# Softmax sums of attention on VectorE, one-bank PSUM slots and shared SBUF slots in a four-layer graph network on one core

## The chip, the cores and the metric

The kernel runs on one core of a Trainium2 chip. The metric is the device time of one execution in microseconds. Before the change three runs gave 3714.34, 3720.96 and 3722.38 us; the median is 3720.96 us.

Each core has TensorE (PE: matrix products, fed by weight loads that overlap them), VectorE (DVE), ScalarE (ACT), GpSimd (POOL) and SyncE (SP, which here issues nearly all DMAs). Matrix products are written to PSUM, 8 banks of 2 KB per partition; everything else lies in SBUF.

## The reference

32 graphs of 512 nodes with 256 features pass through four layers. Each layer normalises its input, cuts it at zero, and adds its result to x:

```python
h = jnp.maximum(_layernorm(x, axis=-1), 0.0); x = x + L0(h, adj)  # 4 heads, additive scores
h = jnp.maximum(_layernorm(x, axis=-1), 0.0); x = x + L1(h, adj)  # 1 head, softmax over axis 1
h = jnp.maximum(_layernorm(x, axis=-1), 0.0); x = x + L2(h, adj)  # bilinear scores
h = jnp.maximum(_layernorm(x, axis=-1), 0.0); x = x + L3(h, adj)  # transformer block
```

Layer 3 is the one that matters most here. It has 8 heads of 32 columns:

```python
q, k, v = heads(split(x @ Wqkv.T + bqkv))
scores = where(allowed, einsum('bhqd,bhkd->bhqk', q * scale, k), -inf)
attn = softmax(scores, axis=-1)
ctx = einsum('bhqk,bhkd->bhqd', attn, v)
x = layernorm(x + ctx @ Wo.T + bo) ; x = layernorm(x + relu(x @ W1.T + b1) @ W2.T + b2)
```

A graph therefore has six norms: one before each layer and two inside layer 3.

## The kernel before, in words

Nodes lie in four blocks of 128 partitions. The program is a list of jobs, one list of the same jobs for each graph. A table, `PLACES`, holds one number for each job of a graph, in the order in which the source makes the jobs. Graph b's job i stands at b x 100,000 + PLACES[i], and `carry_out` emits all jobs of all graphs in the order of these places; on each engine this is the order of execution. So the jobs of about five graphs are interleaved, and a "round" of 100,000 places holds every job of one graph's list once, from different graphs. A job is one instruction, except that a call of `matmuls` is one job for a group of products. Each float32 product appears in the trace as two instructions. In the first rounds the later layers' work is not there yet, and in the last rounds the earlier layers' work is gone: these are called fill and drain below.

`WARM` is a second list: at a place it puts a number of products of the identity with a weight, whose results nobody reads (`ps_warm` in the trace). They stand only in the first rounds. Before, there are 78 of them.

Tiles are handed out of slots. `K` says how many slots each kind of tile has, and `carry_out` gives a new tile the slot that has been out of use longest. The eight PSUM banks before: `ps_a`, two slots of one bank; `ps_b`, two slots of two banks; `ps_ct` and `ps_to`, one bank each. In SBUF each kind of tile has its own slots: small numbers of columns aside, 14 slots of 2 KB (p, y, to, inv3), 23 of about 4 KB (x, masks, h, hT, wh and so on) and 6 of 8 KB (adj, rows0, p1, qk and two for p3).

`norm_stats` (L445) does four statistics and four aggregations on VectorE, then the inverse root of the variance: Ln and Exp on ScalarE, three VectorE steps of a Newton iteration, one VectorE check of range into `ok`, and `shift` on VectorE. `normed` applies it with four ScalarE instructions.

In layer 3 (L680) the heads come in two groups of four (loop over g), and for each group the source nodes come in four blocks (loop over j). For one (g, j): four products give the scores `ps_s` of four heads; two ScalarE exponentials of 1024 columns give `p3`; VectorE multiplies it with the mask; then four products with v add to `ps_ct`, and four products with a matrix of ones add to `ps_to`, the sum of the exponentials, spread over the 32 rows of each head. After j = 3 the sums of the first group go through DRAM to be turned into reciprocals in a shape that uses all partitions (`to_d`, `part`, `in_d`, `inv`: four DMAs in a row), and those of the second group are turned directly from PSUM by two VectorE reciprocals of 256 columns. The output projection `wo`, a norm, the feed-forward products (`ps_f`, first f1, then f2), and a last norm follow.

The late weights (13 tensors of layer 3, 16 loads) are put on GpSimd's queue behind the larger of the first two numbers of the table, that is behind the first loads of adjacency and x.

Of the kernel before, what the change touches and what calls it, by code (L numbers as in the profile page):

```python
# [11 lines left out]
F32 = mybir.dt.float32  # L12
# [4 lines left out]
OP = mybir.AluOpType  # L17
# [13 lines left out]
SHIFT = 45.0  # L31

# [250 lines left out]
def width(args):  # L283
# [7 lines left out]
    4941, 0, 45989, 55878, 52736, 53088, 65883, 75806, 126827, 257141, 153885, 318759, 211656, 217633, 19570,  # L291
    1228, 4500, 10919, 22752, 14242, 24780, 24734, 24972, 24973, 27735, 28443, 30996, 28846, 32925, 37040,
    40036, 39571, 47279, 52268, 53574, 53821, 53821, 54654, 43514, 54475, 54475, 54993, 55764, 55984, 55984,
    55984, 55984, 56107, 61238, 61239, 61239, 61239, 61300, 63031, 63709, 66485, 67354, 69503, 62835, 62835,
    67024, 64457, 65078, 68506, 69270, 74656, 76682, 80285, 83989, 77078, 81039, 86599, 86599, 86599, 89133,
    89469, 89469, 93130, 79369, 91586, 88558, 103135, 103216, 103216, 104243, 105108, 105108, 98449, 109305,
    108751, 106888, 109305, 109305, 109392, 109476, 111470, 112436, 115065, 110602, 104584, 113822, 117055,
    117056, 128079, 128539, 128539, 128540, 131428, 131985, 131985, 160167, 164815, 157449, 132402, 141909,
    138829, 164636, 146420, 163821, 163940, 170363, 172091, 172091, 178335, 195013, 352413, 196976, 205278,
    205507, 205507, 205507, 205306, 205742, 205742, 205751, 205972, 205777, 205777, 205829, 205829, 208425,  # L300
    213342, 214247, 214247, 208403, 208426, 208428, 210913, 210913, 213654, 209281, 209281, 210044, 218310,
    215531, 233659, 226926, 226927, 233310, 233310, 247338, 251067, 253705, 254637, 234450, 237759, 237759,
    242240, 233549, 235402, 241481, 252228, 239918, 242726, 247267, 254175, 257745, 257745, 257745, 257745,
    257745, 258204, 258204, 258204, 259293, 259293, 330297, 272806, 262275, 257879, 257938, 259931, 260558,
    258171, 257938, 261933, 260558, 262075, 262075, 262075, 265602, 265603, 267573, 265874, 269500, 269793,
    267082, 269953, 270582, 270582, 270871, 271669, 271669, 271613, 271613, 271613, 271805, 271805, 271670,
    273796, 273591, 273796, 273861, 276238, 278300, 279108, 279108, 279109, 279109, 279039, 274044, 276752,
    280924, 276983, 282260, 285040, 285625, 287505, 282260, 281913, 283149, 286565, 284076, 286699, 288031,
    288518, 288143, 281743, 281743, 281743, 282736, 282736, 290598, 302996, 303568, 304126, 289466, 291476,
    293111, 298737, 298738, 299315, 291986, 296584, 296584, 328450, 424820, 304255, 294640, 311427, 316750,  # L310
    316314, 305973, 313426, 317622, 318586, 318586, 319319, 319319, 320472, 317622, 321103, 325728, 328100,
    325395, 326602, 333285, 333285, 333677, 335177, 336098, 336215, 336215, 336215, 336215, 370706, 345694,
    351822, 351822, 351822, 352367, 354547, 353407, 353408, 355772, 355772, 356635, 355773, 341670, 341670,
# [15 lines left out]
]  # L329

WARM = [
    (86598, 15), (103134, 3), (109304, 4), (117054, 3), (143513, 8), (186598, 16), (203134, 3), (243513, 8),
    (253820, 2), (255983, 5), (262834, 2), (270581, 1), (273590, 2), (279107, 2), (281742, 1), (286598, 1),
    (341669, 2),
]
# [1001 lines left out]
```

## Time and profile before

| | |
|---|---|
| median of three runs | 3720.96 us |
| span of the profiled execution | 3722.8 us |
| PE busy | 3638.5 us |
| DVE busy | 2742.9 us |
| ACT busy | 1813.4 us |
| POOL busy | 11.1 us |
| `ps_to` products | 2048 instructions, mean 594 ns |
| `ps_ct` products | 2048 instructions, mean 605 ns |
| mask product `p<-p,m` of 128x2048 | 256 instructions, mean 2284 ns |
| exponential `p<-ps_s` of 128x1024 | 512 instructions, mean 1023 ns |

The profiled execution's span lies 1.8 us above the median. Products of four heads run beside each other in the array, and products are pipelined, so the cost of a group is read from the distance of its start to the next group's start, not from the mean of one instruction. In the busy table a share is of the whole span; in the rows of slices each digit is the busy share of a fortieth of the span in tenths.

### The profile page before, as it was taken

What the parts mean: (1) busy time and instruction counts of PE and PEld (TensorE: products, weight loads), DVE (VectorE), ACT (ScalarE), POOL (GpSimd) and SP (SyncE); (2) the same over time, 40 slices, a digit from 0 to 9 for tenths busy, and PEclk for the clock granted to TensorE, in tenths of its full rate; (3) what the DMA queues carried; (4) which work ended last, traced back from release to release, by engine and by line L of the source; (5) the groups of instructions that cost most, each with busy time, mean ns of one, the idle gap of its engine ahead of it and who ended that gap; (6) DMA issues with size and microseconds to landing.
All of it is one profiled execution on the core that took longest, in us unless ns stands there. A gap on an engine that the chain in (4) does not pass through costs nothing.

```text
span 3722.8 us, 52235 instructions
## 1 busy us (share of the span) xinstructions
PE 3638.5 (98%) x20130; PEld 2376.4 (64%) x20130; DVE 2742.9 (74%) x6267; ACT 1813.4 (49%) x3393; POOL 11.1 (0%) x25
## 2 busy tenths in 40 slices
PE   6899999999999999999999999999999999999986
PEld 5766676666666666666666667666667666666543
DVE  4687777787777787777788777778777778777554
ACT  1255544545544455544455554455554455554443
POOL 1000000000000000000000000000000000000000
PEclk8899999999999999999999999999999999999998
DMA  4111111111111111111111111111111111110000
GB/s 139 40 44 49 30 31 49 45 44 49 32 32 46 45 44 50 32 36 42 45 44 50 32 46 31 45 48 45 33 45 31 47 48 44 43 36 15 15 10 10
DMA packets 152351, 152.75 MB, mean 41 GB/s; under 512 B 87840, under 2 KB 122144, under 8 KB 148000
## 3 DMA queue, kind: packets, MB, share of 16 engines
q1 hardware_dynamic: 149632, 144.35, 13.4%
q0 software_dynamic: 1216, 3.94, 0.3%
q8 instruction: 161, 2.64, 0.3%
q10 hardware_dynamic: 1248, 1.05, 0.1%
q14 instruction: 94, 0.77, 0.1%
HBM read 114.57 MB, written 17.96 MB: 36 GB/s over the span
## 4 chain that ended last, share of the span: by engine, by line
PE 94%; DVE 3%; DMA 1%; ACT 1%; issue 0%; SPq 0%; ACTq 0%; DVEq 0%
PE ps_o L267 24%; PE ps_f L267 24%; PE ps_s L267 7%; PE ps_ct L267 6%; PE ps_wh L267 6%; PE ps_qk L267 6%; PE ps_to L267 6%; PE ps_t L265 4%; PE ps_e L267 4%; PE ps_v L267 3%; PE ps_wo L267 3%; DVE p L214 1%; DMA rows<-rows_d 1%; PE ps_y L265 1%; DVE st L214 0%
## 5 line engine op out<-in xcount | busy, mean ns | idle before, releaser
L267 PE MATMUL ps_o<-wh,p 128*128 128x65 f32 (+1 forms) x5120 | 723.8, 298 | 9.5 <-DVE p L214 9.1
L267 PEld LDWEIGHTS ps_o<-wh,p 128*128 128x128 f32 x5120 | 679.5, 194 | 76.7 <-issue 37.3
L214 DVE TENSOR_TENSOR p<-p,m 128x2048 f32<-128x2048 f32 x256 | 584.7, 2284 | 33.7 <-ACT p L214 33.7
L214 ACT ACTIVATE p<-ps_s 128x1024 f32<-128x1024 f32 x512 | 506.6, 1023 | 183.1 <-PE ps_s L267 182.3
L267 PE MATMUL ps_f<-tT,ff_t 128*128 128x512 f32 x1024 | 456.4, 599 | 2.6 <-ACT tT L214 2.6
L267 PE MATMUL ps_f<-ff_t,f 128*128 128x256 f32 x2048 | 454.1, 380 | 0.0
L267 PEld LDWEIGHTS ps_f<-ff_t,f 128*128 128x128 f32 x2048 | 384.4, 190 | 51.4 <-issue 1.8
L214 DVE SCALAR_TENSOR_TENSOR p<-rows,rt,mT 128x512 f32<-128x512 f32 x512 | 368.4, 738 | 18.3 <-DMA rows<-rows_d 18.3
L214 ACT ACTIVATE h<-x,shift,rstd 128x256 f32<-128x256 f32 x512 | 272.5, 590 | 215.5 <-PE ps_o L267 160.0
L267 PEld LDWEIGHTS ps_f<-tT,ff_t 128*128 128x128 f32 x1024 | 193.9, 192 | 222.6 <-issue 208.7
L267 PE MATMUL ps_s<-qk 32*128 32x512 f32 x2048 | 294.9, 641 | 2.5 <-ACT qk L214 1.4
L214 ACT ACTIVATE f<-ps_f,ff1b_c 128x512 f32<-128x512 f32 x256 | 164.0, 679 | 247.0 <-PE ps_f L267 247.0
L267 PE MATMUL ps_ct<-p,v 128*32 128x512 f32 x2048 | 272.9, 605 | 8.2 <-DVE p L214 7.0
L267 PE MATMUL ps_to<-p,ones 128*32 128x512 f32 x2048 | 267.5, 594 | 0.0
L214 ACT ACTIVATE rstd<-mv,eps 128x4 f32<-128x4 f32 x192 | 56.2, 292 | 432.9 <-DVE mv L214 432.8
L267 PE MATMUL ps_o<-h,p 128*128 128x257 f32 x1024 | 240.4, 387 | 0.0
L267 PE MATMUL ps_qk<-h3T,wqkv_t 128*128 128x512 f32 x512 | 238.3, 593 | 0.0
L267 PEld LDWEIGHTS ps_o<-h,p 128*128 128x128 f32 x1024 | 190.8, 191 | 52.3 <-issue 26.0
L214 DVE TENSOR_TENSOR u<-ps_f,n 128x512 f32<-128x512 f32 x64 | 44.3, 692 | 237.4 <-PE ps_f L267 237.4
L214 DVE BATCH_NORM_STATS2 st<-x 128x6 f32<-128x256 f32 x512 | 204.3, 415 | 9.1 <-DMA x<-in_x_dram 4.7
L267 PEld LDWEIGHTS ps_s<-qk 32*128 32x128 f32 x2048 | 81.4, 183 | 166.3 <-ACT p L214 55.4
L265 PEld LDWEIGHTS ps_t<-ident,h 128*128 128x128 f32 x1024 | 120.3, 142 | 93.5 <-issue 52.3
(133 smaller groups left out, 4489.3 us busy)
## 6 DMA issues: line engine op xcount, KB each, us to landing
adj<-in_adj_dram SPq DMA_DIRECT2D x32, 1024.0 KB
rows<-rows_d SPq DMA_DIRECT2D x32, 1024.0 KB
x<-in_x_dram SPq DMA_DIRECT2D x32, 512.0 KB
rows<-rows_d SPq DMA_DIRECT2D x32, 512.0 KB
out_dram<-y SPq DMA_DIRECT2D x32, 512.0 KB
inv<-in_d SPq DMA_DIRECT2D x32, 256.0 KB
ff_t<-in_L_gnn_W_dram POOLq DMA_DIRECT2D x2, 1024.0 KB, 11.8
mT<-m SPq DMA_TRANSPOSE x128
```

What stands on the lines that cost most here:

```text
L214: return [getattr(unit, method)(*map(real, args), **{k: real(v) for k, v in kw.items()})]
L265: made.append(self.nc.tensor.transpose(*map(real, c)))
L267: made.append(self.nc.tensor.matmul(*map(real, c[:3]), start=c[3], stop=c[4]))
```

## The change

The sums of the exponentials move: VectorE adds the four masked tiles of a head group into one tile `acc` (three additions of 128x2048), and one group of four products with ones turns `acc` into `ps_to`. The reciprocals of both head groups now go through DRAM. All PSUM tiles share eight slots of one bank; score tiles, projections and feed-forward tiles are made one bank wide, so an exponential now takes 512 columns and there are four per (g, j). SBUF tiles of layer and kind share slots by size: 9 of 8 KB, 19 of 4 KB, 8 of 2 KB. The inverse root is two GpSimd instructions (add, power of -0.5), without Newton steps. Range checks are gathered in one tile `seen` per graph and done by three instructions. Several steps go from VectorE to ScalarE: the mask tile `m`, the first half of the transposed copies, the layer 0 products `wh` (now one per head), and the layer 2 products `ha`. The adjacency of a graph is now issued ahead of its x. The whole table of places is new, and `WARM` has 276 products in 25 places.

Places in the new table that are spoken of below: adjacency load 0, x load 29304, first root of x 63434, `h0` transposes 70775 and after, scores of layer 3 from 385313 to 416057, the last sum 424877, ones-products 410801 and 427148, output projection 432396 to 440859, feed-forward products 448926 to 476873. (A place of 385313 is place 85313 of a graph's fourth round.)

```diff
-            adj=1, x=3, mT=3, m3=3, h0=1, h0T=1, wh0=1, rows0=1, e0=1, p=6,
-            h1=1, h1T=1, wh1=1, rows1=1, p1=1, y=4, x2=2,
-            h3=1, hT3=1, qk=1, vt=1, p3=2, to=2, inv3=2, n=1,
-            kinds=2, rt0=2, rt1=2, inv2=2, part=4,
...
-    K |= {"ps_ct": Kind(psum, "ps_ct", 1), "ps_to": Kind(psum, "ps_to", 1)}
-    K |= {"ps_a": Kind(psum, "ps_a", 2), "ps_b": Kind(psum, "ps_b", 2)}
+    SHARED = dict(
+        big="adj rows0 p1 qk p3 acc",
+        mid="x x2 mT m3 e0 h0 h0T wh0 h1 h1T wh1 rows1 h3 hT3 vt n",
+        half="p y to inv3",
+    )
+    K = {tag: Kind(act, tag, slots) for tag, slots in dict(big=9, mid=19, half=8).items()}
+    K |= {"ps": Kind(psum, "ps", 8)}
...
-        plan.act("activation", rstd, mv[:, :, 1], AF.Ln, bias=eps, fixed=0.27)
-        plan.act("activation", rstd, rstd, AF.Exp, scale=-0.5)
-        r = new("newton", "newton", [P, NT])
-        plan.dve("scalar_tensor_tensor", r, mv[:, :, 1], EPS, rstd, OP.add, OP.mult)
-        plan.dve("scalar_tensor_tensor", r, r, -0.5, rstd, OP.mult, OP.mult)
-        plan.dve("scalar_tensor_tensor", rstd, r, 1.5, rstd, OP.add, OP.mult)
-        plan.dve("scalar_tensor_tensor", ok[:, :NT], mv[:, :, 1], 2.0**60, ok[:, :NT], OP.is_le, OP.mult)
+        ve = new("ve", "ve", [P, NT])
+        plan.pool("tensor_scalar_add", ve, mv[:, :, 1], EPS, fixed=0.6)
+        plan.pool("tensor_tensor", rstd, ve, nhalf, OP.pow, fixed=0.6)
...
-        plan.dve("tensor_scalar_max", m, adj_t, 0, each=0.52e-3)
+        plan.act("activation", m, adj_t, AF.Relu, fixed=0.5)
...
-            if k % 2:
-                plan.act("copy", hT[:, k], to_sbuf)
-            else:
-                plan.dve("tensor_copy", hT[:, k], to_sbuf)
+            plan.act("copy", hT[:, k], to_sbuf)
...
-            plan.dve(
-                "tensor_mul",
-                wh[:, i, :, :F0],
-                ps[:, :D].split("p (h f) -> p h f", (H0, F0), h=H0),
-                wh[:, i, :, F0 : F0 + 1].flat(lambda t: t.to_broadcast([P, H0, F0])),
-            )
+            for hd in range(H0):
+                plan.act("mul", wh[:, i, hd, :F0], ps[:, cut(hd, F0)], wh[:, i, hd, F0 : F0 + 1], fixed=0.28)
...
-            plan.dve(
-                "tensor_scalar_mul", ha_k[k], hT[:, k].split("p (a b) -> p a b", (2, D), a=2), a2_t[:, k : k + 1],
-                each=0.52e-3, fixed=0.2,
-            )
+            plan.act(
+                "mul", ha_k[k], hT[:, k].split("p (a b) -> p a b", (2, D), a=2), a2_t[:, k : k + 1], fixed=0.28
+            )
...
+            acc = new("acc", "acc", [P, HG, N])
             for j in range(NT):
-                ps = [new("ps_b", "ps_s", [P, 2, N]) for _ in range(HG // 2)]
+                ps = [new("ps", "ps_s", [P, N]) for _ in range(HG)]
...
-                for q in range(HG // 2):
-                    plan.act("activation", p[:, 2 * q : 2 * q + 2], ps[q], AF.Exp)
+                for r in range(HG):
+                    plan.act("activation", p[:, r], ps[r], AF.Exp)
                 plan.dve("tensor_mul", p, p, m3[:, j : j + 1].flat(lambda t: t.to_broadcast([P, HG, N])))
...
-                    *((ps_to[at], ones, p[:, r], j == 0, j == NT - 1) for r, at in enumerate(heads)),
                 )
+                if j == 0:
+                    first_p = p
+                else:
+                    plan.dve("tensor_add", acc, acc if j > 1 else first_p, p)
+            ps_to = new("ps", "ps_to", [P, N])
+            plan.matmuls(0.882, *((ps_to[at], ones, acc[:, r], True, True) for r, at in enumerate(heads)))
             inv = new("inv3", "inv3", [P, N])
-            if last:
-                for half in (slice(0, N // 2), slice(N // 2, N)):
-                    plan.dve("reciprocal", inv[:, half], ps_to[:, half], each=7.5e-3, fixed=0.13)
-                    plan.dve("tensor_mul", cT[:, g, half], ps_ct[:, half], inv[:, half])
...
-            if not last:
-                plan.act("copy", cT[:, g], ps_ct)
+            plan.act("copy", cT[:, g], ps_ct)
...
+    def all_within(seen, mv):
+        for n, bound, what in ((UPPER, RANGE, OP.is_le), (BOTH, 1.0 / RANGE, OP.is_ge)):
+            plan.dve("scalar_tensor_tensor", ok[:, :n], seen[:, :n], bound, ok[:, :n], what, OP.mult)
+        to = ok[:, : 6 * NT].rearrange("p (k t) -> p k t", k=6)
+        plan.dve("scalar_tensor_tensor", to, mv[:, :, :, 1], 2.0**60, to, OP.is_le, OP.mult)
```

## The prediction

> **What bounds the kernel now.** I read the page's busy table and its slices first, then the busy time by stage, then the chain of work that ended last in order of time, and last the matrix products of one stretch.
>
> ```profile
> span 3722.8 us, 52235 instructions
> PE 3638.5 (98%) x20130; PEld 2376.4 (64%) x20130; DVE 2742.9 (74%) x6267; ACT 1813.4 (49%) x3393; POOL 11.1 (0%) x25
> PE   6899999999999999999999999999999999999986
> PEclk8899999999999999999999999999999999999998
> ```
> TensorE is busy 98% of the span, at full clock except in the first and last slices. The stages say how exactly:
>
> ```profile
> 0.00:250.00 250.00, 210.95 (x1106) 158.65 (x1106) 154.23 (x383) 81.72 (x174) 11.08 (x25) 0.90 0.25 77
> 1000.00:1500.00 500.00, 499.63 (x2874) 326.08 (x2867) 391.17 (x883) 252.44 (x474) 0.00 (x0) 1.00 0.16 44
> 1500.00:2000.00 500.00, 499.92 (x2747) 326.81 (x2749) 376.27 (x874) 256.48 (x481) 0.00 (x0) 1.00 0.14 39
> 3400.00:3723.00 323.00, 278.26 (x1338) 157.26 (x1336) 174.69 (x359) 133.17 (x219) 0.00 (x0) 0.94 0.04 13
> ```
> (Columns: stretch, its length, busy time of PE, weight loads, DVE, ACT, POOL, then granted clock, DMA share, GB/s.) In mid-run PE lacks 0.45 us in 1000. It waits only while the pipeline fills (39 us of the first 250) and drains (45 of the last 323). The same products come once per graph in the chain:
>
> ```profile
> 2029.70 8.94 PE ps_o L267 x56
> 2140.75 8.94 PE ps_o L267 x56
> ```
> so a graph costs 111.05 us, all of it PE's. 32 graphs are 3553.6 us; the other 169 us are the fill's and drain's waits (84), the filler products (41.5) and the low clock at both ends (0.10 of 250 us and 0.06 of 323, together 44). What a ones-product costs is read from the starts:
>
> ```profile
> 2012.96 1.06 PE L267 MATMUL ps_ct<-p,v 128*32 128x512 f32 x8
> 2013.84 1.04 PE L267 MATMUL ps_to<-p,ones 128*32 128x512 f32 x8
> 2014.81 1.14 PE L267 MATMUL ps_s<-qk 32*128 32x512 f32 x8
> ```
> From `ps_ct` to `ps_to` is 0.88 us; from `ps_to` to the other shape 0.97, of which 0.09 is the change of shape and stays with `ps_ct` once `ps_to` is gone.
>
> **The change, part by part.**
>
> *Ones-products.* Eight groups per graph become two: 6 x 0.88 x 32 = 169 us off PE, on the path since PE has no waits. By the table's new order the `ct` groups stand in 3 runs instead of 7 (4 x 0.09 saved), but PE changes between kinds of product 74 times a round instead of 61; 13 changes cost between 0 and 0.09 each. That is -0.4 to +0.8 us per graph; I take 0, as most of the new changes are between products of one shape. New cost: 105.8 us a graph.
>
> *VectorE.* Added: 6 sums per graph of the shape of `p<-p,m` (2284 ns): 192 x 2.284 = 438.5. `part` and `cT` for the second head group, 32 x (0.246 + 0.685) = 29.8; three checks, 96 x about 0.18 = 17. Removed, by their rows: `m<-adj` 39.1, three transposed copies 65.6, `wh` products 53.1, `ha` 31.1, Newton 90.9, the `ok` rows 89.6, reciprocals from PSUM 112.2, `cT<-ps_ct` 26.2: 507.8. Net -23, so 84.5 us per graph of 105.8. The load is moved, not raised, but where it lies matters (third rival).
>
> *ScalarE.* Added: `m` 32 x 1.99 = 64; copies 96 x 0.587 = 56; 512 `wh` products of 64 columns at about 0.25 (between 171 ns for 4 and 504 for 256 columns) = 128; `ha` 64 x 0.69 = 44; exponentials 1024 x 0.598 - 506.6 = 106; copies of `cT` 19 and split copies 11. Removed: the two root steps, 96. Net +332, to 2145 us, some 59% of the new span: off the path, hidden by PE's products. If that cover went, 10 us per graph would show.
>
> *Roots on GpSimd.* Two small instructions per norm replace Ln, Exp and three Newton steps, which took from 3672.22 (last statistic) to 3673.39 before `shift`. No POOL arithmetic is in this trace in mid-run. Nearest rows: a memset of one column, 98 ns, below; a DMA issue, 0.9 us, above. A pair is 0.2 to 1.8 us against 1.17, so -1.0 to +0.6 per norm and a hand-over or two; I take 0.5 an instruction, in the middle, as neither row is arithmetic, and so no change. Queued behind a root are `shift`, four norm steps and the transposes; in mid-run PE has the feed-forward products in front of those.
>
> The Trainium skill ("SBUF — State Buffer", SBUF: two separate sides) speaks against this step: a GpSimd instruction that reads SBUF and a VectorE instruction with two SBUF inputs exclude each other for their whole length. No row here shows it. By it a root could wait for one 2.28 us sum, and VectorE would lose the twelve short instructions of a graph, an estimated 6 us at the 0.5 above: the sum below would stay, since 6 is under VectorE's slack, but the third rival would come nearer.
>
> *POOL's queue at the start.* The first graph's root stands at place 63434, the late weight loads at 29305. In the trace those loads hold POOL from 5.93 to 24.13 us, and the first transposes ran at 14.25. The first root comes at 24.1 or later, then `shift`, one norm step of 0.59 and the transposes: 26 to 29 us. Bounds 0 (were PE held by something else) to +15; I take +12. This contains that x is now read behind the adjacency and that `m` and `kinds` (2 us each) stand ahead of the norm on ScalarE.
>
> *Filler products.* 78 become 276, 396 more instructions. Over this trace's mean (41.5/156 = 0.266) that is 105 us; at full clock (32 in 7.07 us, 0.221) 88. They run in PE's order whatever PE would do otherwise. They can stand in waits that the trace shows: 39 us in the fill less the first 14, before any product. So +63 to +105; I take 80. The new order explains them: in rounds 1 to 3 there are no feed-forward products yet, and `h0`'s transposes (place 70775) stand where those would cover a chain of VectorE steps.
>
> *Drain.* For the second head group the sums' reciprocal goes through DRAM instead of 2 x 1.75 us from PSUM. At the end of the trace the first `to` group ended its trip with steps of 1.7 us (issue of `to_d` 3663.28, of `part` 3664.97). Four such hops, copy 0.585, reciprocal 0.246 and product 0.685 make 8.3 us against the 2.3 that PE waited there: +6 on the last graph, 0 to +6 on the two before it, plus one 2.28 us sum in front of each: +8 to +25; I take 15. In mid-run `o2`, `wh1` and `o0` products of other graphs, which the table puts between `to` and `wo`, hide it. The two more DMA starts (0.32 and 0.55 us) lie on SP, which idles 32 us a round (2032.9 to 2065.2); behind them wait the `rows` of layer 1 and the mask transposes.
>
> *Buffers.* PSUM: the same eight banks; PE waited about 2 us in all for a slot's reader, so there is little to gain; single banks free sooner. SBUF: 14 slots of half size become 8, 23 of middle size 19, the large ones 9 from 6. A later reader now delays a writer more. Bounds 0 to the third rival; I take 0.3 us per graph, 10 us.
>
> Sum against the profiled execution: 3722.8 - 169 + 80 + 12 + 15 + 10 = 3671. The median of the three runs, 3720.96, is 2 us under that execution; I say 3670.
>
> **Rivals.**
>
> *The ends cost little* (18%): fillers 63, start and drain 0, no waits: 3617. For it: fillers also keep the clock up (0.81 between 14 and 50 us). Against: POOL's queue at the start.
>
> *PE's gain comes back as small waits everywhere, no change* (6%): 3714 to 3728.
>
> *VectorE becomes the bound where the heads run: slower* (20%). By the table VectorE has its work of one round between place 85,000 and place 65,000 of the next, and almost none while the feed-forward runs. Counting rows by place, 76.7 of its 84.5 us lie there, beside 84.2 of PE's 105.8: it may lose 7.5 us per graph before PE waits. Of the waits in this trace, those on steps that stay (exponentials 33.7, `e` 68.1, `ps_y` 28.3, `ps_o` 73.4) make 203/32 = 6.4 us per graph. Its wait for `rstd` before the Newton steps, 66/32 = 2.1, becomes one for GpSimd before `shift`; twice as long, it is 4. Together 10.4, so 2.9 too many: 93 us, 3754 in place of 3661 without the 10. It decides from 9.4 lost us per graph (1.9 us of waiting, 62 us in all). For it: sums stand right behind the mask products in VectorE's order. Against: a PE that is later lets VectorE stop waiting for PE, and VectorE then loses less than in this trace.
>
> **How the numbers follow.** The likeliest case has 56%, 3670, by itself 3630 to 3712. Range: half of the slower rival lies above 3755 and a quarter of the cheap-ends rival below 3605, with some of the likeliest's tails: 3605 to 3755. A change within 0.2% (7 us) can't be told from none with these runs. Faster 0.56 + 0.18 = 0.74, same 0.06, slower 0.20.
>
> **What would show it.** Right: `ps_to` with 512 instructions and the same chain step 105 to 107 us apart; PE dense in mid-run; the fill some 90 us longer with filler products in it; first transposes near 27 us; DVE about 84 us per graph. Wrong: PE waiting for `DVE p` or `acc` in mid-run (third rival), roots of over 1 us, or fillers that cost less than 60 us.

## The result and the profile after

After the change four runs give 3863.04 to 3864.74 us, median 3863.52; the kernel before, run beside it, 3717.89 (3714.34 to 3722.38). The ratio is 1.0392, with a 95% interval of 1.0377 to 1.0407: 3.9% slower, where 1.4% faster was forecast (3670 against 3720.96). It lies 108.5 us above the end of the range.

The page of the changed kernel, the same lines as were shown of before:

```profile
span 3863.0 us, 50373 instructions
...
PE 3595.0 (93%) x18990; PEld 2426.5 (63%) x18990; DVE 2758.2 (71%) x5083; ACT 2031.3 (53%) x4321; POOL 344.8 (9%) x409
...
PE   6999999999999999999999999999999999999885
...
PEclk9999999999999999999999999999999999999987
```

TensorE did lose work: 43 us of busy time and 1,140 instructions (1,536 of ones-products less, 396 of fillers more). But it is no longer dense. The busy time by stage (stretch, length, busy time of PE, weight loads, DVE, ACT, POOL, then clock, DMA share, GB/s):

```profile
0.00:250.00 250.00, 218.11 (x1204) 192.82 (x1205) 96.31 (x255) 73.62 (x182) 22.23 (x41) 1.00 0.25 71
1000.00:1500.00 500.00, 479.61 (x2518) 323.17 (x2518) 373.06 (x715) 281.15 (x595) 48.21 (x56) 0.99 0.14 40
1500.00:2000.00 500.00, 473.86 (x2568) 311.51 (x2566) 384.34 (x674) 285.26 (x612) 46.64 (x52) 0.99 0.16 44
3400.00:3863.00 463.00, 382.09 (x1767) 231.55 (x1765) 270.80 (x440) 197.52 (x394) 31.72 (x38) 0.91 0.05 16
```

Before, PE lacked 0.45 us in the 1000 us of the two middle stretches; now it lacks 46.5. How long a round is, is best read over many of them: each graph ends with one output DMA. In the timeline of that DMA, between 600 and 3450 us, 26 of them start (first and last start at the end of the line), of the kernel before:

```profile
L235 SPq DMA_DIRECT2D out_dram<-y x26: 388/432/1287, 671.1 to 3424.2; - x26
```

and of the changed kernel:

```profile
L236 SPq DMA_DIRECT2D out_dram<-y x26: 383/433/1169, 607.6 to 3441.5; - x26
```

So a round is 2753.1 / 25 = 110.12 us before and 2833.9 / 25 = 113.36 after. Taken this way, 32 rounds leave 3722.8 - 3523.8 = 199 us for fill and drain before, and 3863.0 - 3627.5 = 235.5 after. Rounds became 3.24 us longer (104 us in all) and the ends 36.5 us; the two make the 140 us between the profiled executions. The prediction had rounds 5.0 us shorter (169 - 10 over 32) and ends 107 us longer. So the ends came out 70 us better than forecast, and the rounds 263 us worse.

The same timeline over the whole span, before and after, gives the first output:

```profile
L235 SPq DMA_DIRECT2D out_dram<-y x32: 388/432/1287, 338.0 to 3715.2; - x32
L236 SPq DMA_DIRECT2D out_dram<-y x32: 383/433/1169, 380.1 to 3855.2; - x32
```

It leaves 42.1 us later, so the growth of the ends is one of the fill.

What PE waits for in mid-run, the groups of PE between 500 and 3400 us of the changed kernel (busy, mean ns | idle before them and what ended it):

```profile
L268 PE MATMUL ps_o<-wh,p 128*128 128x65 f32 (+1 forms) x4128 | 594.9, 296 | 11.5 <-DVE p L215 11.2
...
L266 PE MATMUL ps_t<-ident,h 128*128 128x128 f32 x808 | 141.9, 278 | 16.2 <-ACT h L215 14.9
...
L268 PE MATMUL ps_wo<-wo_t,cT 128*128 128x256 f32 x416 | 118.4, 424 | 54.7 <-DVE cT L215 54.6
...
L268 PE MATMUL ps_to<-acc,ones 128*32 128x512 f32 x416 | 55.4, 601 | 20.4 <-DVE acc L215 17.6 <-ACT y L215 1.8 <-ACT p L215 0.8
...
L266 PE MATMUL ps_y<-ident,y 128*128 128x128 f32 x156 | 31.4, 291 | 38.1 <-DVE y L215 38.1
```

Four of the five end with a VectorE result. Waits for `p` and `acc` were named beforehand as the sign of the third rival; they are 29 of the 144 us that PE idles here, `cT` and `y` are 93. VectorE's own groups in the same stretch show what it stands in:

```profile
L215 DVE SCALAR_TENSOR_TENSOR p<-rows,seen,mT 128x512 f32<-128x512 f32 x415 | 295.2, 741 | 73.2 <-DMA rows<-rows_d 73.2
...
L215 DVE SCALAR_TENSOR_TENSOR p<-rows,seen,mc 128x512 f32<-128x512 f32 x103 | 76.0, 738 | 49.4 <-ACT seen L215 49.4
...
L215 DVE TENSOR_TENSOR cT<-cT,inv 128x512 f32<-128x512 f32 x52 | 36.0, 692 | 130.3 <-DMA inv<-in_d 123.2 <-ACT wh L215 7.1
L215 DVE TENSOR_TENSOR u<-ps_f,n 128x512 f32<-128x512 f32 x50 | 34.1, 682 | 237.8 <-PE ps_f L268 237.8
...
L215 DVE TENSOR_TENSOR y<-y,g_r 128x1024 f32<-128x1024 f32 x25 | 30.6, 1226 | 43.6 <-ACT y L215 43.6
...
L215 DVE SCALAR_TENSOR_TENSOR shift<-mv,rstd 128x4 f32<-128x4 f32 x151 | 24.4, 162 | 124.6 <-POOL rstd L215 124.6
```

In the kernel before, the same stretch and view:

```profile
L214 DVE TENSOR_TENSOR u<-ps_f,n 128x512 f32<-128x512 f32 x52 | 36.0, 692 | 163.0 <-PE ps_f L267 163.0
...
L214 DVE TENSOR_TENSOR cT<-cT,inv 128x512 f32<-128x512 f32 x26 | 17.8, 685 | 0.0
...
L214 DVE COPY spr<-ps_sp 8x128 f32<-8x128 f32 (+1 forms) x53 | 14.6, 275 | 191.8 <-PE ps_sp L265 191.8
```

Before, VectorE's two largest waits were for PE: it was ahead, and while PE is dense such a wait costs nothing. After, only the wait for the feed-forward (`u`) is one for PE. The five others (421 us, 16.5 per round) are for DMAs, GpSimd and ScalarE, that is for hand-overs of chains in which VectorE itself is a link. VectorE is about as busy as before: 2201.86 us in 25.58 rounds are 86.1 per round, against 84.3.

### The profile page after: what moved, and what is told of

Read it like the earlier page. It is cut to its first block, busy times and chain, and to the rows that moved or that the text cites. A ratio compares the mean times of both kernels' runs of the same rounds, so it can differ in the third digit from the quotient of the medians.

```text
span 3863.0 us, 50373 instructions
## 1 busy us (share of the span) xinstructions
PE 3595.0 (93%) x18990; PEld 2426.5 (63%) x18990; DVE 2758.2 (71%) x5083; ACT 2031.3 (53%) x4321; POOL 344.8 (9%) x409
## 4 chain that ended last, share of the span: by engine, by line
issue 56%; DVE 18%; PE 10%; POOL 8%; DMA 6%; ACT 2%; POOLq 0%; DVEq 0%; SPq 0%; ACTq 0%
DVE p L215 7%; POOL rstd L215 5%; PE ps_o L268 4%; POOL ve L215 3%; DMA inv<-in_d 3%; PE ps_warm L268 2%; DVE acc L215 2%; DVE n L215 2%; DMA rows<-rows_d 2%; DVE x L215 1%; DVE st L215 1%; PE ps_wo L268 1%; DVE m L215 1%; ACT n L215 1%; DVE mc L215 1%
## 5 line engine op out<-in xcount | busy, mean ns | idle before, releaser
L268 PE MATMUL ps_o<-wh,p 128*128 128x65 f32 (+1 forms) x5120 | 738.0, 296 | 12.9 <-DVE p L215 12.6
L215 ACT ACTIVATE p<-ps_s 128x512 f32<-128x512 f32 x1024 | 554.6, 607 | 63.2 <-PE ps_s L268 62.4
L268 PE MATMUL ps_f<-ff_t,f 128*128 128x256 f32 x2048 | 480.7, 379 | 0.0
L215 DVE SCALAR_TENSOR_TENSOR p<-rows,seen,mT 128x512 f32<-128x512 f32 x512 | 363.7, 741 | 107.6 <-DMA rows<-rows_d 95.9
L215 POOL TENSOR_SCALAR ve<-mv 128x4 f32<-128x4 f32 x192 | 120.3, 627 | 3476.0 <-DVE mv L215 3472.2
L215 ACT ACTIVATE n<-t,shift,rstd 128x256 f32<-128x256 f32 x128 | 66.4, 589 | 525.9 <-DVE shift L215 525.9
L215 DVE TENSOR_TENSOR acc<-acc,p 128x2048 f32<-128x2048 f32 x128 | 291.9, 2281 | 2.2
L268 PE MATMUL ps_ct<-p,v 128*32 128x512 f32 x2048 | 241.6, 600 | 10.0 <-DVE p L215 10.0
L266 PE MATMUL ps_t<-ident,h 128*128 128x128 f32 x1024 | 180.6, 279 | 54.7 <-ACT h L215 53.1
L268 PE MATMUL ps_wo<-wo_t,cT 128*128 128x256 f32 x512 | 150.8, 436 | 81.1 <-DVE cT L215 81.1
```

The source lines that it names most:

```text
L215: return [getattr(unit, method)(*map(real, args), **{k: real(v) for k, v in kw.items()})]
L266: made.append(self.nc.tensor.transpose(*map(real, c)))
L268: made.append(self.nc.tensor.matmul(*map(real, c[:3]), start=c[3], stop=c[4]))
```

## The experiments

Rounds below are read from the output DMA as above; busy and idle time per round are those of the stretch 500 to 3400 us over the number of rounds in it.

| kernel | time, us | round | PE busy | PE idle | DVE busy | DVE idle |
|---|---|---|---|---|---|---|
| before | 3717.9 | 110.1 | 110.1 | 0.0 | 84.3 | 25.9 |
| after | 3863.5 | 113.4 | 107.7 | 5.6 | 86.1 | 27.3 |
| e1 direct reciprocals | 3845.8 | 113.3 | 107.5 | 5.8 | 89.5 | 23.8 |
| e2 roots on ScalarE | 3821.0 | 112.8 | 108.0 | 4.8 | 85.6 | 27.2 |
| e3 no additions | 3680.1 | 107.2 | 105.1 | 2.1 | 72.5 | 34.7 |
| e4 no fillers | 3838.6 | 113.0 | 107.3 | 5.6 | 85.7 | 27.2 |
| e5 sums undone | 3845.9 | 113.0 | 111.0 | 2.1 | 73.4 | 39.6 |
| e6 two additions of three | 3805.5 | 111.1 | 108.2 | 2.9 | 81.6 | 29.5 |
| e7 before, with sums alone | 4095.2 | 123.2 | 112.1 | 11.1 | 98.0 | 25.2 |
| e8 = e6, e2 and e4 | 3731.6 | 109.3 | 107.1 | 2.2 | 80.7 | 28.6 |
| e9 = e8 and e1 | 3760.4 | 111.4 | 108.6 | 2.8 | 84.8 | 26.6 |
| e11 without n's scale and shift | 3852.3 | 112.9 | 107.5 | 5.4 | 83.4 | 29.5 |
| e12 = e9, copy of sums later | 3710.7 | 108.9 | 106.4 | 2.5 | 83.9 | 25.0 |
| e13 = e12, all additions | 3809.5 | 113.1 | 107.6 | 5.5 | 89.0 | 24.1 |

The changed kernel's four runs lie within 2 us, but the five, ten and twelve runs of e9, e12 and e14 spread over 24 to 26 us, and the other variants have one run each. So differences in time of some 25 us or less prove little by themselves; the readings below rest on rounds, waits and the time of the first output in the traces.

### e3: the additions left out

```diff
-                if j == 0:
-                    first_p = p
-                else:
-                    plan.dve("tensor_add", acc, acc if j > 1 else first_p, p)
+                acc = p
...
```

> The changed kernel without the six additions per graph: the ones-product takes only the last block of nodes, so the softmax sums are not the reference's; nothing else is changed. VectorE loses 13.7 us of work a round. Serial-loop theory and VectorE-load theory: PE has no waits left, the round is PE's 107.1 us: 3670 to 3700. Roots theory: within 30 us of 3863. If the products' own time is what grew, PE stays at 107 busy us a round and this shows it without waits.

Measured: 3680.07 us. One line of the stages, 500 to 3400 us:

```profile
500.00:3400.00 2900.00, 2843.55 (x15473) 1929.69 (x15475) 1961.60 (x4082) 1689.48 (x3600) 230.41 (x322) 1.00 0.16 44
```

Without the six additions (13.7 us of VectorE per graph) the round is 107.2 us, 6.2 less than after. PE is dense but for one wait, 50.6 us for `cT`. The time lies in the range that both theories of VectorE gave, and far from the roots theory. The products that are left keep PE busy 105.1 us a round: the price of the ones-products was forecast well. It is the additions that hide it. This edit also frees the slots of `acc`; e13, below, changes the additions and keeps `acc`.

### e2: the roots back on ScalarE

```diff
-        plan.pool("tensor_scalar_add", ve, mv[:, :, 1], EPS, fixed=0.6)
-        plan.pool("tensor_tensor", rstd, ve, nhalf, OP.pow, fixed=0.6)
+        plan.act("activation", rstd, mv[:, :, 1], AF.Ln, bias=eps, fixed=0.27)
+        plan.act("activation", rstd, rstd, AF.Exp, scale=-0.5)
```

(No Newton steps; GpSimd has no arithmetic left.)

> The changed kernel with the roots back on ScalarE: Ln and Exp, without the Newton steps (so the root has only the tables' accuracy) and without GpSimd. Serial-loop theory: VectorE waits 4.8 us a round for roots; Ln and Exp take about 0.6 with hand-over where GpSimd's pair takes 1.4 and up to 3.3, so three norms in the chain give 2 to 4 us a round: 3735 to 3800. VectorE-load theory: no VectorE work is taken away, within 20 us of 3863. Roots theory: the whole 5.4 us of PE waits goes: about 3690.

Measured: 3820.96 us, 42.6 less, in none of the three ranges. The wait for `rstd` fell from 124.6 us to 51.4 in the stretch, but the round only from 113.36 to 112.80, and 20 us of the gain are at the start (the first output left at 360.4 us, not 380.1). So the roots are a cost, not the cause: the round gave 0.56 us where the roots theory wanted 5.4. With GpSimd gone the chain of waits can be followed through mid-run, and shows one whole round of the loop:

```profile
2001.07 19.35 PE ps_f L268 x58
...
2052.44 1.39 ACT h L215 x3
2053.83 6.04 DMA rows<-rows_d
2059.90 4.29 DVE p L215 x4
2064.22 2.29 DVE acc L215
...
2079.13 2.25 DVE acc L215
2081.38 2.20 DVE p L215
2083.74 2.17 DVE acc L215
2086.05 1.06 PE ps_to L268 x8
...
2095.65 4.67 DMA inv<-in_d
2100.41 0.70 DVE cT L215
2101.15 4.54 PE ps_wo L268 x12
...
2113.62 19.35 PE ps_f L268 x58
```

Between the two lines of 19.35 us lie 112.55 us. PE's products set the first 44 (feed-forward, projections, scores); then a norm and the trip of `rows` through DRAM (15 us), VectorE's stretch of masks and sums from 2059.90 to 2086.05, the trip of the sums and the output projection, and the feed-forward again. PE is busy most of that time, but it isn't PE that sets it: VectorE cannot run ahead, since it waits for `rows` at its head and for the feed-forward at its end.

### e5 and e6: the sums undone, and one addition in three undone

```diff
+                    *((ps_to[at], ones, p[:, r], j == 0, j == NT - 1) for r, at in enumerate(heads)),
...
-                if j == 0:
-                    first_p = p
-                else:
-                    plan.dve("tensor_add", acc, acc if j > 1 else first_p, p)
...
-            plan.matmuls(0.882, *((ps_to[at], ones, acc[:, r], True, True) for r, at in enumerate(heads)))
```

```diff
-                else:
+                elif j < NT - 1:
                     plan.dve("tensor_add", acc, acc if j > 1 else first_p, p)
...
+                *((ps_to[at], ones, acc[:, r], True, False) for r, at in enumerate(heads)),
+                *((ps_to[at], ones, p[:, r], False, True) for r, at in enumerate(heads)),
```

(e6 keeps two additions per head group, four per graph.)

> The changed kernel with its sums alone undone: the six additions per graph are gone, and a ones-product follows each block again (eight groups per graph into one slot of PSUM per head group); table, slots, roots and fillers stay as changed. Theory (VectorE's work among the heads sets the round): VectorE has 13.7 us per graph less, so PE sets the round: 107.65 us, the round measured without the additions, plus 6 x 0.88 = 112.9; the ends as there, 235 us: 3848 us, between 3825 and 3865. The sums then bring next to nothing in this order of work. Rival (PE's waits in mid-run have nothing to do with VectorE's load, and the sums do save PE 5.3 us per graph): the waits stay and PE's work comes back: 3863 + 32 x 5.3 = 4033 us, above 3960.

> The changed kernel with the last addition of each head group left out of VectorE: two additions per group make the sum of three blocks, and the ones-products add the fourth block themselves (four groups per graph, not two). Sums are complete. VectorE does 2 x 2.28 = 4.6 us per graph less, PE 2 x 0.88 = 1.8 us more. Theory (VectorE's work among the heads sets the round, one for one): the round is the larger of PE's 107.65 + 1.8 = 109.4 and 113.2 - 4.6 = 108.6: 109.4 and some tenths: 3745 us, between 3725 and 3790. Rival (the round is set by PE's work and by waits that do not depend on VectorE's load): 3863 + 32 x 1.8 = 3920 us.

Measured: 3845.89 us, as the theory had it, and 3805.45 us, above the theory's 3790. In this order of work the sums on VectorE gain nothing against eight groups of ones-products on PE: with the sums undone PE has 5.3 us a round more to do and the round is still 0.3 shorter. PE then sets it, with one wait (e5):

```profile
500.00:3400.00 2900.00, 2847.36 (x16035) 1880.37 (x16034) 1883.40 (x3908) 1619.12 (x3441) 219.31 (x306) 1.00 0.15 43
L285 PE MATMUL ps_wo<-wo_t,cT 128*128 128x256 f32 x416 | 110.2, 400 | 45.3 <-DVE cT L232 45.3
```

e5 also shows what the rest of the change costs: without any sum on VectorE it is still 125 us slower than the kernel before. By the profiled executions its rounds are 2.9 us longer, 93 us in all, and its ends 29 us. In a round PE idles 2.1 us more, 1.8 of them the wait for `cT` behind the second head group's trip through DRAM, and is busy 0.9 us more, which is unexplained. So the sums eat up the gain that was forecast for them; most of the loss against the kernel before comes from the other parts.

The best lies between: with two additions of three on VectorE (e6) the round is 111.1. Its loop is still there, since PE's own 107.0 (105.1 and a wait of 1.9, as in e3) and 1.8 would make 108.8. Taking away 4.6 us of VectorE's work gave 2.2 us, half of what the theory of one-for-one asked; that PE got 1.8 more may be a part of the reason.

### e7: the sums alone, in the kernel before

```diff
+                product = p if j else acc
-                plan.dve("tensor_mul", p, p, m3[:, j : j + 1].flat(lambda t: t.to_broadcast([P, HG, N])))
+                plan.dve("tensor_mul", product, p, m3[:, j : j + 1].flat(lambda t: t.to_broadcast([P, HG, N])))
...
-                    *((ps_to[at], ones, p[:, r], j == 0, j == NT - 1) for r, at in enumerate(heads)),
...
+                if j:
+                    plan.stand(SUMS[g][j - 1]).dve("tensor_add", acc, acc, p)
+            plan.stand(ONES[g]).matmuls(0.882, *((ps_to[at], ones, acc[:, r], True, True) for r, at in enumerate(heads)))
```

(`stand` gives a job a place outside the table; SBUF slots shared by size.)

> The kernel before with the sums alone: three additions of 128x2048 per head group on VectorE (acc is the product of block 0, the other three are added), one group of ones-products per head group; the table of places of before, with the additions right behind the products with v of their block and the first head group's ones-product and its copy some 3,000 places later; reciprocals of the second group from PSUM, roots, PSUM slots and fillers as before. To make room for two acc tiles the SBUF slots are shared by size (8 of 8 KB, 19 of 4 KB, 13 of 2 KB). PE's work falls by 5.3 us per graph to 105.8, VectorE's rises by 13.7 to 99.4. Theory (VectorE's work among the heads sets the round): VectorE had 25 us of room per graph before and keeps 6.4, less than the waits it has in its stretch, so the gain is partly or wholly lost: 3620 to 3740 us. Rival (it is the new table and the other parts that cost the time, the sums as such gain 169 us): 3545 to 3585 us.

Measured: 4095.16 us, far over both. The line of its stages:

```profile
500.00:3400.00 2900.00, 2638.06 (x13566) 1729.59 (x13559) 2305.70 (x4750) 1330.23 (x2497) 0.00 (x0) 0.96 0.13 37
```

VectorE is busy 98.0 us a round, 13.7 more than before, as it should be, and idle 25.2, about as much as before (25.9). The work came on top of the waits, and the round grew by 13.1. Before, I had read those 25.9 us as room because VectorE waited for PE in them (`spr` 191.8). It still waits there for 170.2 us, although now PE waits for VectorE too (77.9 us at `ps_y`, 71.5 at `ps_t`): in a loop both engines wait, and neither wait is room. With the new table and the other moves the same sums come to rounds of 113.4 us. The slots differ here too, so how much of the 13.1 is due to them stays open, as does the part of the granted clock, 0.96 here.

### e11: VectorE's work away from the heads

```diff
-        plan.dve("tensor_mul", n, n, g1_r.unsqueeze(1).to_broadcast([P, NT, D]))
-        plan.dve("tensor_add", n, n, b1_r.unsqueeze(1).to_broadcast([P, NT, D]))
...
```

> The changed kernel without the two VectorE products of n with ln1_g and ln1_b (n*g1 and n+b1, 2 x 1.22 us per graph; that scaling and shift of the residual is left out, nothing else). They stand in VectorE's order at places 55,095 and 56,292 of a round, behind the heads and ahead of the stretch in which VectorE waits some 9 us for the feed-forward products. Theory (only VectorE's work among the heads, up to t, sets the round): nothing is gained, 3855 to 3866 us; VectorE's wait for ps_f grows by about 2.4 us a round. Rival (VectorE's whole load sets the round): 2.4 x 32 = 78 us less, 3785 us.

Measured: 3852.28 us, 11 less; of 2.4 us a round less work 0.46 came back (e4 and e10, which change nothing in mid-run, have rounds shorter by 0.40 and 0.59). VectorE's wait for the feed-forward took up the rest:

```profile
L232 DVE TENSOR_TENSOR u<-ps_f,n 128x512 f32<-128x512 f32 x50 | 34.1, 682 | 297.8 <-PE ps_f L285 297.8
```

It was 237.8, and is 2.3 us a round longer. So it matters where VectorE's work lies, not its load as a whole: work in front of the wait for the feed-forward is nearly free, work among the heads, between the trip of `rows` and the output projection, is not.

### e1, e9, e12 and e14: the second head group's reciprocals from PSUM

```diff
+            if g == KD - 1:
...
+                for half, where in ((slice(0, N // 2), 428380), (slice(N // 2, N), 428382)):
+                    plan.stand(where).dve("reciprocal", inv[:, half], ps_to[:, half], each=7.5e-3, fixed=0.13)
+                    plan.stand(where + 1).dve("tensor_mul", cT[:, g, half], ps_ct[:, half], inv[:, half])
+                continue
             plan.act("copy", cT[:, g], ps_ct)
```

> The changed kernel, but the second head group's sums are turned into reciprocals straight from PSUM, as before the change (two VectorE reciprocals of 256 columns and two products, some 4.3 us, in place of four DMAs, two copies' worth of waiting and one product). Serial-loop theory: one chain per round (u, VectorE's stretch with the heads, ones-product, reciprocals, wo, norm, feed-forward, u) sets the round of 112.7 us; this takes PE's wait for cT (2.1 us a round) and a part of VectorE's waits for inv (4.8) out of it, so the round falls by 2 to 5 us, to 108 to 110.5, and the time from 3863 to 3700 to 3795. VectorE-load theory: only VectorE's work counts, 3 us more of it a round makes 3863 into 3900 to 3960. Roots theory: GpSimd's roots alone cost the round its 5.4 us of PE waits; within 20 us of 3863.

Measured: 3845.78 us, with the round unchanged at 113.3. The time is within the 20 us of the roots theory, but e2 speaks against that theory; the other two missed. PE no longer waits for `wo`, but for a slot of PSUM that the reciprocals still read:

```profile
L285 PE MATMUL ps_wh<-w_t,h1T 128*128 128x258 f32 x416 | 117.9, 420 | 74.2 <-DVE inv L232 74.2
...
L285 PE MATMUL ps_wo<-wo_t,cT 128*128 128x256 f32 x416 | 100.2, 384 | 0.0
```

The same on top of three other edits (e8, below):

> The changed kernel with four edits: the three of the run before (last addition of each head group left to the ones-products, roots by Ln and Exp, no fillers; 3731.6 us together, rounds of 109.3 us) and the second head group's reciprocals read directly from PSUM. There PE's only large wait in mid-run was for cT, 57.4 us in 2900, 2.2 us per round, behind the four DMA hops of the second head group. Theory (VectorE has some us of room per round once one addition per group is gone, so a wait that is taken away stays away): the hops leave the path, VectorE works 2.9 us per graph more within its room, rounds of 107 to 108: 3731 - 70 + the drain's hops saved, some 10: 3650 to 3700 us. Rival (as with the direct reciprocals alone, VectorE is late and the wait turns into one for the PSUM slot that the reciprocals hold): 3715 to 3735 us.

Measured: 3760.42 us (3736.40 to 3761.04 in five runs), above both ranges and slower than without the direct reciprocals. Here a new wait appeared on VectorE, 3.0 us a round, for ScalarE's copy of the sums, which the table puts first:

```profile
L232 DVE RECIPROCAL inv<-ps_to 128x256 f32<-128x256 f32 x53 | 92.8, 1751 | 77.3 <-ACT to L232 77.3
```

e12 puts that copy behind the reciprocals (place 431,244 in place of 428,159, with its two DMAs):

> The run with four edits (e9: last additions to the ones-products, Ln and Exp, no fillers, direct reciprocals of the second head group; rounds of 111.4 us) with one hand-over taken away: ScalarE's copy of the second group's sums, and the two DMAs behind it that only feed the range check, are placed behind the reciprocals (431,244 in place of 428,159). In e9 VectorE waited for that copy before its reciprocal 77.3 us in 2900, 2.9 us per round, and PE waited 2.8 us per round for the reciprocals' slot. Theory of waits (hand-overs on VectorE are what is left on the loop): both go, rounds of 107 to 109 us: 3760 - 25 x 3 = 3670 to 3700 us. Theory of work (VectorE's work among the heads sets the round, a wait taken away is used up by the next): 3735 to 3760 us.

Measured: 3710.70 us, ratio to before 0.9993 (0.9975 to 1.0011). The hand-over was worth 50 us, between the two forecasts; the slot's wait stayed (66.4 us). e14 moves two groups of `wh1` products behind the `o2` products on PE:

```diff
-    219032, 219570, 229915, 230329, 230937, 222514, 222929, 223537, 222100, 223344, 233250, 221685, 232808,
+    219032, 219570, 231240, 231241, 231245, 222514, 222929, 223537, 222100, 223344, 233250, 221685, 232808,
```

> The run e12 with two groups of layer-1 products (wh1 of block 0) and their copy moved on PE behind the 1.74 us of o2 products that followed them (places 231,240 and 231,241 in place of 229,915 and 230,329; the copy at 231,245). In e12 these wh1 products waited 66.4 us in 2900, 2.5 us per round, for the PSUM slot that the second group's reciprocals and products hold. Theory (the wait ends at a fixed time after the sums, and work put in front of it covers it): 1.7 us per round go, rounds of 107.2: 3655 us, between 3640 and 3680. Rival (VectorE is late there and the products moved ahead wait for it in their turn): within 12 us of 3711.

Measured: 3711.47 us, ratio 0.9983 (0.9969 to 0.9997). The wait went from the one group of products to the other:

```profile
L285 PE MATMUL ps_o<-h,p 128*128 128x257 f32 x854 | 218.2, 399 | 68.9 <-DVE cT L232 68.9
```

The products in front did not cover it, as the rival had it: VectorE's order, not PE's, sets when those slots come free.

### e8 and e13: edits together, and work against waits

e8 is e6 with the roots of e2 and no fillers.

> The changed kernel with three edits together: the last addition of each head group left to the ones-products, roots by ScalarE's Ln and Exp without Newton steps, no fillers. Theory: what each is worth adds up where it lies in different places: 3863 - 118 (round 113.1 to 109.4) - 25 (fillers, measured alone) and, of the 42 measured alone for the roots, the part at the start, some 10 to 20, as the rounds are PE's by then: 3700 to 3725 us, about the time before. Rival (the edits take from the same wait, so that only the largest counts): 3740 to 3800 us.

Measured: 3731.62 us. The round is 109.3, which is PE's own 107.1 and one wait, 57.4 us in 2900 for `cT`. So the edits do add up: 132 us, against 58, 43 and 25 one by one. (The time lies between the two ranges, 7 us from the first.)

> The same, with all three additions per head group on VectorE again (as the change has them), so VectorE does 4.6 us per graph more than in e12 and PE 1.8 us less. Theory of waits: VectorE's work still fits once the hand-over is gone, and PE's saving counts: some 50 us below e12, 3620 to 3660 us. Theory of work: 4.6 us of VectorE's work per round come back as time, less what room e12 leaves: 40 to 120 us above e12.

Measured: 3809.47 us, 99 above e12. Two additions a graph more, and the round goes from 108.9 to 113.1: 4.2 us for 4.56 us of VectorE's work, although PE has 1.8 less to do. That is the theory of work, nearly one for one, and against the theory of waits. The tile `acc` and its slots are there in both kernels, so it is the additions and not the slots that cost the time. The two stage lines, e12 first:

```profile
500.00:3400.00 2900.00, 2833.62 (x15650) 1915.48 (x15649) 2234.00 (x4197) 1694.07 (x3836) 0.00 (x0) 1.00 0.15 41
```

and e13:

```profile
500.00:3400.00 2900.00, 2759.98 (x14741) 1868.03 (x14738) 2281.64 (x4123) 1649.22 (x3722) 0.00 (x0) 0.98 0.15 40
```

### e4 and e10: the start

```diff
-WARM = [
-    (74379, 1), (76448, 1), (96586, 8), (113750, 29), (133222, 11), (141270, 8), (170774, 36), (174379, 1),
...
-]
+WARM = []
```

> The changed kernel without any filler product. Fillers on the path: they take 124 us of PE's time in the first 243 us and PE has no wait there, so without them the time falls by 60 to 124 us, to 3740 to 3800, less what a lower clock costs. Fillers in waits: the fill is as long as VectorE's, ScalarE's and the DMAs' chains make it and the time stays within 25 us of 3863, or rises with a lower clock.

Measured: 3838.55 us, 25 less. The fillers are busy 124.2 us, all within the first 250, but without them the first output leaves only 9.8 us earlier (370.3 instead of 380.1). The rest stood in waits that are there without them, or came back as clock: the granted clock of the first 250 us is 0.75 without fillers and 1.00 with them. How much is which was not separated. The other 15 us of the 25 come after the first output.

```diff
-    plan.aside(max(PLACES[:2]) + 1)
+    plan.aside(64600)
```

> The changed kernel with the late weight loads placed behind the first root of x on GpSimd's queue (place 64600 in place of 29305); nothing else. Theory (the loads hold the first root: in the changed kernel's trace the last one is issued at 28.04 and the root runs at 29.83, while x landed at 11.5): the first transposes move from 31.8 to some 16 to 18 us, and 12 to 15 us come off: 3848 to 3852 us. Rival (fillers and later chains set the end of the fill, whatever the first root does): within 4 us of 3863.5.

Measured: 3840.03 us, 23.5 less. The timeline of the first transposes in the changed kernel (first and last start among those before 120 us):

```profile
L266 PE MATMUL ps_t<-ident,h x23: 272/273/473, 31.8 to 119.1; 128*128 128x128 f32 x23
```

and with the loads behind the first root:

```profile
L266 PE MATMUL ps_t<-ident,h x24: 272/273/477, 17.1 to 105.7; 128*128 128x128 f32 x24
```

They come 14.7 us earlier, and so does the first output (365.1, 15.0 earlier). The other 9 us come in the rounds behind it, which are 112.77 us instead of 113.36, with the same 5.6 us of PE waits and 0.55 us less PE busy time. Why was not settled.

## Why the prediction was wrong

*Ones-products: right as a price, not as a gain.* The products left on PE take 105.1 us a round (e3) where 105.8 was forecast. The forecast's base of 111.05 us was a single step of the chain; the mean of 25 rounds is 110.12, and 110.12 - 5.28 is 104.8. (With that mean the ends before are 199 us, not 169; that the three parts named added up to 169 was chance.) But a saving on PE becomes time only while PE sets the round, and after the change it doesn't.

*VectorE: 84.5 us forecast, 86.1 measured.* The load was nearly right (the forecast's own rows make (2742.9 - 23) / 32 = 85.0). "The load is moved, not raised, but where it lies matters" named the point, and the sum then left it at nothing for the likeliest case. This is the step that failed: all of the 169 us was taken as "on the path since PE has no waits", and new waits in mid-run were put at 0.3 us a graph (the 10 us for the buffers). In the changed kernel PE waits 5.6 us a round. Of the 263 us that the rounds missed, 197 go with the additions (113.36 - 107.20, e3, times 32). The other 66 are there without them (107.20 where the forecast saving from the measured mean gives 105.15), 60 of them the wait for `cT`. The third rival, given 20%, was what happened.

*The third rival itself: right mechanism, less than half the price.* It put 2.9 us a round on VectorE's being late, 93 us. Measured against PE's 105.1 and its one wait of 1.9, the additions cost 6.2 us a round (113.36 - 107.20), 197 us. Term by term: VectorE's work 84.5 forecast, 86.1 measured; its idle time beside the feed-forward 21.6 - 7.8 = 13.8 forecast, 9.3 measured; all its other waits 10.4 forecast, 18.0 measured. The last is what was mis-sized. The forecast kept the waits of the trace before (exponentials, `e`, `ps_y`, `ps_o`: 6.4) and added one for the roots (4, measured 4.9). The kept ones nearly all went, as its "against" foresaw: those for the exponentials are 6.9 us in the stretch (12.1 before). In their place came waits that the trace before hardly shows: `inv` 123.2 us (0.0 before), `rows` 73.2 (1.9), `seen` 49.4, `y` 43.6 (0.0); 289 us in 25.58 rounds, 11.3 per round. Each is a step that stands in VectorE's order behind a trip through DRAM (`inv`, `rows`) or a ScalarE step (`seen`, `y`) that now comes later than VectorE.

*Roots on GpSimd: small, but dearer than taken.* 0.23 us for an undisturbed addition, 1.04 for an undisturbed power, against 0.5 each; 42.6 us in all against ScalarE without Newton steps (e2), of which 19.7 come before the first output. "Roots of over 1 us" was named as a sign of a wrong prediction.

*POOL's queue at the start: right mechanism, about the right size.* First transposes at 31.8 us where 26 to 29 was forecast; worth 15.0 us at the first output (e10) where 12 was forecast, and 23.5 in all.

*Filler products: much too dear.* 80 us on the path was forecast; without them 9.8 us go before the first output and 25 in all (e4). The step took the waits that they can stand in as 25 us, from the old trace; of their 124.2 us in the new order all but some 10 to 25 were covered by waits or came back as clock.

*Drain.* The +15 was not measured alone. The ends as a whole grew by 36.5 us and the first output by 42.1, so nothing is left for it. Fillers, loads and roots, taken out one at a time, bring the first output 9.8, 15.0 and 19.7 us forward, 44.5 in sum: that is the growth, from other terms than the forecast's. "In mid-run products of other graphs hide it" was wrong: the second head group's trip makes PE wait for `cT` 54.6 us in the stretch, 2.1 us a round, and even in e3, with VectorE relieved, 1.9.

*Buffers.* PE waited for no slot worth naming in the changed kernel. That PSUM slots can bind showed only with the direct reciprocals (66 to 86 us in the stretch). More SBUF slots were not tried.

*ScalarE.* 2031 us, not 2145. Half of the difference is that exponentials that follow each other overlap: 554.6 us of busy time for 1024 of 607 ns, where 612 were forecast. It was off the path either way.

The range ended at 3755 because half of the slower rival was cut off there, and that rival's own price had no range: had the waits been bounded by "as many as the VectorE idle time of before", 25.9 us, the sum would have been 84.5 + 25.9 = 110.4 us a round, 3533 us for 32 rounds, and with ends of 169 + 107 us 3809.

## What to carry to other kernels

Work moved from the busiest engine to one that is 74% busy is not free while that engine stands in the loop of the steps: in these kernels VectorE's idle time stayed between 23.8 and 29.5 us a round wherever it set the pace (25.2 in e7, 27.3 after, 24.1 in e13), so its room is not the round less its work. The idle time alone doesn't tell which engine sets the pace, either: in the kernel before, where PE does, it is 25.9. Before such a move, follow one round of the chain, count what each engine must do between its first late input and its last needed output, and hold that against the round. A split that leaves a part of the work on the old engine can do better than either end, as e6 did here; and a wait taken away on PE can come back at the next hand-over from VectorE, as in e1 and e14. None of the kernels here that computes the whole result is clearly faster than the one before: e12 and e14, with four edits and more, are level with it.

## What the runs showed of the hardware that I had not expected

A GpSimd instruction on 128x4 elements can last over nine times its usual length when VectorE works beside it. The timeline of the changed kernel:

```profile
2074.95 2.26 DVE L215 TENSOR_TENSOR acc<-p,p 128x2048 f32<-128x2048 f32 x1
2075.13 2.17 POOL L215 TENSOR_SCALAR ve<-mv 128x4 f32<-128x4 f32 x1 [3.10 <-DVE mv L215]
...
2077.39 1.04 POOL L215 TENSOR_TENSOR rstd<-ve,nhalf 128x4 f32<-128x4 f32 x1
```

The addition took 2.17 us where the median is 0.23, and it ended 0.09 us after VectorE's sum. The rule of the Trainium skill ("SBUF — State Buffer", SBUF: two separate sides), that a GpSimd instruction and a VectorE one with two SBUF inputs exclude each other for their whole length, agrees with this row. An addition that ran beside `x<-ps_o,e`, with one input in SBUF and one in PSUM, took its usual 0.23 us (at 2070.68). The wait adds to the roots of the changed kernel, since the sums and mask products, 2.28 us each, are the longest instructions on VectorE: the mean of all 192 GpSimd additions is 627 ns.

The granted clock also differs in mid-run: 1.00 in the kernel before and in e3, 0.99 in the changed kernel, 0.96 in e7, where PE idles 11 us a round. So waits of PE may cost more than their length; no run separates the two. The sum of the waits alone doesn't set it: e4, with 5.6 us of them a round, ran at 1.00, and e2, with 4.8, at 0.98. Nor does the clock explain PE's busy time, which is 105.1 us a round in e3, but 107.7 in the changed kernel and 107.3 in e4 for the same products. That stays open.
